# Attention block on one core: half of two units inverted on VectorE, query weights and pair sums moved

## The chip, the cores and the metric

The kernel runs on one core of a Trainium2 chip. The metric is the device time of one execution in microseconds. The engines are named as in the profile: PE (TensorE, matmuls), DVE (VectorE), ACT (ScalarE), POOL (GpSimd) and SP (SyncE, which issues DMAs). PE writes to PSUM, from which DVE and ACT read; POOL works in SBUF alone.

## The reference

Layer 0 is a convolution with a selective scan; layer 1 is an attention and then a recurrence over tokens. The change touches the attention only:

```python
t = t + _L1_attn_ref(_ln_t(t), Wt, Wx, bh, Wa, ba)   # t: 4 batches x 4096 tokens x 128

q = jnp.einsum('bld,ud->blu', x, Wt)                  # u = 32
k = jnp.einsum('bld,ud->blu', x, Wx)
beta = jnp.tanh(q[:, :, None, :] + k[:, None, :, :] + bh)
alpha = jnp.einsum('bsju,u->bsj', beta, Wa[:, 0]) + ba[0]
alpha = jnp.tanh(alpha)
alpha = jax.nn.softmax(alpha, axis=-1)
c_r = jnp.einsum('bsj,bjd->bsd', alpha, x)
```

For each pair of a query and a key the score is a weighted sum of 32 tanh values. There are 4 x 4096 x 4096 such pairs.

## The kernel before, in words

The attention is `_rational`. It groups the 32 units into six sets of five or six. Within a set, the sum of tanh values is one quotient N/D of two sums over products of exponentials, which matmuls form from a query factor `E` and a key factor `F`. So a pair costs six quotients, not 32 tanh. D is the product of `F` and `E` ("lower", tile `pd`), and N that of `F` and `cE`, which is `E` times a constant per row (`weigh`, L1379; the constants hold the factor `LOWER`, 2^-13).

**Tiling.** A block is 512 queries (QB) of one batch against all 4096 keys: 4 batches x 8 blocks = 32 blocks. Its 32 key tiles (`jt`) hold 128 keys each. A key tile has three units, "A", "B1" and "B2" (in odd tiles A, B2, B1), each with two halves (two of the six sets), so a unit is 2 x 512 columns. Unit (30,0) is the A unit of key tile 30, and the numbers 0, 1, 2 are the units' places in the tile.

**The loop over units (L1520 to L1548).** The instructions are written in a fixed order by hand (`manual_schedule`), and every engine takes its own in that order. At step i:

- ACT takes the logarithm of unit i's denominators out of PSUM (Ln, L1524) and then the exponential of unit i-1's negated logarithm (Exp, L1527). Together they invert D.
- DVE multiplies unit i-2 by its numerators, half by half (`times`, L1414: one input in SBUF, one in PSUM).
- POOL adds a B unit's two quotients to those of the tile's A unit (L1533), two adds per key tile.
- At the step in which a tile's first B unit is multiplied, DVE adds the two halves of the tile before into the scores `A` (`whole`, L1518; both inputs and the output in SBUF).
- PE forms the denominators of unit i+2 and the numerators of unit i-1 (L1393).

The buffers that tie these together: two PSUM tiles `pd` for denominators (each a whole unit), three banks `pn` for numerators (each half a unit), one bank `ct` for everything else; four `ra` tiles for A quotients and five `rb` tiles for B quotients.

**Between the units.** The dictionary `between` holds extra steps by (key tile, place), run after that unit's instructions: the norm of the next batch (14 to 23), the last 12 value matmuls of the block before (2 to 13), its closing division (14 to 21, with the residual add L1462 on POOL), the next block's query factors (23 to 26: matmul, maximum on DVE, exponential L1300 on ACT), and in the first block of a batch the transposes of the values (24 to 30).

**The tanh stretch.** At a block's end ACT loads another table and computes tanh and exp of the scores in four parts, the last over key tiles 20 to 31 (L1583, L1584). Before it, DVE weighs the next block's `E` into `cE`. Meanwhile `ahead` does key tile 0 of the next block without ACT: `direct` inverts D on DVE by a reciprocal (L1424) and multiplies by N (L1425). It also forms the first two denominators of key tile 1 (`first`). Then ACT loads its table again (L1266) and the next block's loop starts at key tile 1. At a change of batch the key factor `F` is first made anew (`all_keys`). DMAs of the stage (SP's queue) fetch one block's residual and, up to the third batch, the next batch's tokens.

The functions as they stand:

Of the kernel before, what the change touches and what calls it, by code (L numbers as in the profile page):

```python
# [8 lines left out]
F32 = mybir.dt.float32  # L9
AF = mybir.ActivationFunctionType  # L10
# [5 lines left out]
P = 128  # L16
# [54 lines left out]
LOWER = 2.0**-13  # L71
TOPS = B * 2 * 2 * (L // QB)
# [1169 lines left out]
def _rational(ctx, tc, k, x1, xn1, x2, top, kept, ba):  # L1242
# [14 lines left out]
    rb = ctx.enter_context(tc.tile_pool(name="nrb", bufs=5))  # L1257
    two = ctx.enter_context(tc.tile_pool(name="ntwo", bufs=2))
    fp = ctx.enter_context(tc.tile_pool(name="nf", bufs=1))
# [116 lines left out]
    def weigh(E):  # L1376
        cE = one.tile([P, 2, QB], F32, name="cE")
        for i in range(2):
            nc.vector.tensor_scalar(cE[:, i, :], E[:, i, :], c_n[:, i : i + 1], None, ALU.mult)  # L1379
        return cE  # L1380
# [31 lines left out]
    def times(r, ns):  # L1412
        for a in range(2):
            nc.vector.tensor_tensor(r[:, a, :], r[:, a, :], ns[a], ALU.mult)  # L1414
# [5 lines left out]
    def direct(d, ns, unit, then=None):  # L1420

        r = ratio(unit)
        for a in range(2):
            nc.vector.reciprocal(r[:, a, :], d[:, a, :])  # L1424
            nc.vector.scalar_tensor_tensor(r[:, a, :], r[:, a, :], 1.0 / LOWER, ns[a], ALU.mult, ALU.mult)  # L1425
            if then is not None:
                then()
                then = None
        return r
# [4 lines left out]
    def later(between, jt, pos, steps):  # L1434
        n = 3 * jt + pos
        for go, after in steps:
            between.setdefault(divmod(n + after, 3), []).append(go)
# [53 lines left out]
    for b in range(B):  # L1491
        upcoming = None
        for s in range(nq):
# [11 lines left out]
            if more:  # L1505
                E_next = two.tile([P, 2, QB], F32, name="E")
                of = upcoming if turned else xn
                for i in range(2):
                    later(between, 23 + 2 * i, 2, zip(queries(E_next, of, (s + 1) % nq, i), (0, 1, 2)))
            ln_exp()  # L1510
            units = [(jt, pos, unit) for jt in range(start, JT) for pos, unit in enumerate(order(jt))]
            n = len(units)
            D = dict(enumerate(first))
            N, R = {}, {}

# [4 lines left out]
            for i in range(n + 2):  # L1520
                if i < n:
                    jt, pos, unit = units[i]
                    r = R[jt, pos] = ratio(unit)
                    nc.scalar.activation(r, D.pop(i), AF.Ln, scale=LOWER)  # L1524
                if 1 <= i <= n:
                    r = R[units[i - 1][:2]]
                    nc.scalar.activation(r, r, AF.Exp, scale=-1.0)  # L1527
                if i >= 2:
                    at, p, unit = units[i - 2]
                    r = R[at, p]  # L1530
                    times(r, N.pop(i - 2))
                    if p:
                        nc.gpsimd.tensor_tensor(R[at, 0], R[at, 0], R.pop((at, p)), ALU.add)  # L1533
                    if p == 1 and at > start:
                        whole(at - 1)
                forms = []
                if i + 2 < n:
                    D[i + 2] = pd()
                    forms.append(halves((D[i + 2][:, 0, :], D[i + 2][:, 1, :]), units[i + 2], F, E))
# [12 lines left out]
            if more:  # L1552
                E, cE = E_next, weigh(E_next)
# [7 lines left out]
            held = {}  # L1561

            def ahead(step):
                if not more:
                    if step == 0:
                        whole(JT - 1)
                    return
                if step == 0:
                    held["A"], held["B1"] = lower("A", F, 0, E), lower("B1", F, 0, E)
                    held["A"] = direct(held["A"], upper("A", F, 0, cE), "A", lambda: whole(JT - 1))  # L1570
# [8 lines left out]
                else:  # L1579
                    held["first"] = held["first"], lower("B2", F, 1, E)  # L1580

# [282 lines left out]
```

## Time and profile before

| what | us |
|---|---|
| median of three runs | 10636.88 (10631.07 to 10638.2) |
| the profiled execution's own time | 10622.87 |
| its span, first to last instruction | 10621.1 |
| attention, first weighing to last table load for tanh | 3611.6 to 10357.8 |
| one block early on, table load to table load | 6330.39 to 6538.47: 208.1 |
| one block of the last batch | 9506.21 to 9717.83: 211.6 |
| Ln and Exp on ACT, sum of the four groups' lengths over the kernel | 7425.0 |
| pool adds of quotients (L1533) on POOL | 5000.9, 2.519 each |

The lengths of ACT's rows overlap, since the next instruction is shown as started before the last has ended. Their sum is more than the stage, so ACT's pace is read from starts. In timelines "x2" is two instructions of the same kind in a row, merged, and "[0.49 <-PE pn L1393]" is idle time before the instruction and what ended it.

### The profile page before, as it was taken

The page shows a single profiled execution, that of the slowest core. Times are in us where ns is not written, and L with a number is a line of the kernel's source. Part 1 is how long each engine was busy: PE and PEld are TensorE (multiplying, and loading weights), DVE is VectorE, ACT ScalarE, POOL GpSimd, SP SyncE. Part 2 cuts the span into 40 slices and gives each one's busy share as a digit, 9 for nine tenths or more (in the row PEclk, how much of TensorE's full clock was granted, in tenths as well). Part 3 has the DMA queues.
Part 4 walks back from the last instruction along what each step waited for, and adds up shares of the span by engine and source line. Part 5 has one row for each costly group of instructions (what it writes and reads, how often), then busy time and mean ns, then how long its engine had stood idle before and what let it go on. Part 6 is the DMA issues. An engine that isn't in the chain of part 4 may idle for free.

```text
span 10621.1 us, 110120 instructions
## 1 busy us (share of the span) xinstructions
PE 9213.9 (87%) x35452; PEld 3226.5 (30%) x35452; DVE 9043.7 (85%) x10031; ACT 9094.5 (86%) x10279; POOL 8609.3 (81%) x3686
## 2 busy tenths in 40 slices
PE   7787787787777799999999999999999999999997
PEld 2121221222211233333333333333333333333334
DVE  7999999999999788888888888888888888888882
ACT  4566666766766799999999999999999999999995
POOL 7999899999999777788678778877888777767773
PEclk8898898898888999999999999999999999999998
DMA  6889889888888200000000000000000000000001
GB/s 150 200 191 213 189 193 212 194 197 209 198 199 203 71 4 4 4 4 7 4 4 4 7 4 4 7 4 4 4 7 4 4 3 5 3 3 3 5 2 66
DMA packets 228573, 739.50 MB, mean 70 GB/s; under 512 B 41536, under 2 KB 42368, under 8 KB 226448
## 3 DMA queue, kind: packets, MB, share of 16 engines
q1 hardware_dynamic: 224576, 730.76, 29.2%
q8 instruction: 280, 4.59, 0.2%
q14 instruction: 309, 2.53, 0.1%
q10 hardware_dynamic: 3408, 1.63, 0.1%
HBM read 609.15 MB, written 118.88 MB: 69 GB/s over the span
## 4 chain that ended last, share of the span: by engine, by line
PE 35%; ACT 21%; DVE 5%; issue 5%; POOL 1%; DMA 0%; DVEq 0%; POOLq 0%; ACTq 0%; SPq 0%
PE pd L1393 16%; PE pn L1393 10%; PE ct L1557 6%; ACT rb L1527 6%; ACT rb L1524 6%; ACT ra L1524 2%; ACT A L1583 2%; DVE rb L1414 2%; ACT ra L1527 2%; ACT A L1584 1%; DVE ra L1424 1%; PE vy L1758 1%; POOL ra L1533 0%; DVE cE L1379 0%; ACT E L1300 0%
## 5 line engine op out<-in xcount | busy, mean ns | idle before, releaser
L1533 POOL TENSOR_TENSOR ra<-ra,rb 128x1024 f32<-128x1024 f32 x1986 | 5000.9, 2519 | 813.0 <-ACT rb L1527 446.5
L1393 PE MATMUL pn<-cE,F 32*128 32x512 f32 (+1 forms) x12288 | 4602.5, 643 | 88.3 <-DVE rb L1414 78.0
L1393 PE MATMUL pd<-E,F 32*128 32x512 f32 (+1 forms) x12288 | 4037.8, 650 | 342.9 <-ACT ra L1524 239.8
L1414 DVE TENSOR_TENSOR rb<-rb,pn 128x512 f32<-128x512 f32 x3972 | 2543.4, 682 | 582.4 <-PE pn L1393 576.8
L1527 ACT ACTIVATE rb<-rb 128x1024 f32<-128x1024 f32 x1986 | 2513.6, 1270 | 0.0
L1524 ACT ACTIVATE rb<-pd 128x1024 f32<-128x1024 f32 x1986 | 2443.0, 1230 | 26.9 <-PE pd L1393 24.6
L786 POOL TENSOR_TENSOR dBu<-dtdu,bbcc 128x1024 f32<-128x1024 f32 x1024 | 2391.4, 2365 | 88.8 <-DMA dtdu<-dd 58.2
L1393 PEld LDWEIGHTS pd<-E,F 32*128 32x128 f32 (+1 forms) x12288 | 1209.9, 186 | 2257.2 <-ACT ra L1524 972.1
L1393 PEld LDWEIGHTS pn<-cE,F 32*128 32x128 f32 (+1 forms) x12288 | 1420.9, 186 | 1317.3 <-DVE rb L1414 647.0
L1414 DVE TENSOR_TENSOR ra<-ra,pn 128x512 f32<-128x512 f32 x1986 | 1356.1, 686 | 384.8 <-PE pn L1393 287.4
L826 PE MATMUL py<-h,gather 128*32 128x512 f32 x4096 | 1190.6, 677 | 391.7 <-POOL h L812 372.9
L1527 ACT ACTIVATE ra<-ra 128x1024 f32<-128x1024 f32 x993 | 1258.0, 1267 | 0.0
L1524 ACT ACTIVATE ra<-pd 128x1024 f32<-128x1024 f32 x993 | 1210.4, 1219 | 52.6 <-PE pd L1393 43.7
L781 ACT ACTIVATE pa<-dtdu,a_neg 128x1024 f32<-128x1024 f32 x1024 | 1143.6, 1117 | 34.7 <-DMA dtdu<-dd 11.2
L802 DVE TENSOR_TENSOR_SCAN pa<-pa,carry,dBu 128x1024 f32<-128x1024 f32 x480 | 1125.4, 2345 | 32.3 <-ACT pa L781 22.9
L1557 PE MATMUL ct<-A,xT 128*128 128x512 f32 x2048 | 1046.4, 639 | 10.5 <-ACT A L1584 10.5
L812 POOL TENSOR_TENSOR h<-h,bbcc 128x1024 f32<-128x1024 f32 x381 | 899.3, 2360 | 121.8 <-ACT carry L810 104.9
L810 ACT COPY carry<-pa 128x1 f32<-128x1 f32 x643 | 103.0, 160 | 883.9 <-DVE h L809 883.3
L809 DVE TENSOR_TENSOR h<-pa,bbcc 128x1024 f32<-128x1024 f32 x643 | 787.7, 1225 | 61.7 <-PE py L826 1.7
L1518 DVE TENSOR_TENSOR A<-ra 128x512 f32<-128x512 f32 x993 | 753.9, 759 | 35.9 <-POOL ra L1533 31.6
L802 DVE TENSOR_TENSOR_SCAN h<-pa,carry,dBu 128x1024 f32<-128x1024 f32 x288 | 673.2, 2341 | 21.3 <-PE py L826 10.6
L826 PEld LDWEIGHTS py<-h,gather 128*32 128x32 f32 x4096 | 221.8, 116 | 1255.9 <-issue 529.0
(306 smaller groups left out, 8282.2 us busy)
## 6 DMA issues: line engine op xcount, KB each, us to landing
bbcc<-bcd SPq DMA_DIRECT2D x1024, 256.0 KB, 7.7
dtdu<-ddd SPq DMA_DIRECT2D x1008, 256.0 KB, 7.8
ddd<-dd SPq DMA_DIRECT2D x63, 1024.0 KB, 5.1
src<-src SPq DMA_DIRECT2D x60, 512.0 KB, 9.7
xs<-in_x_dram SPq DMA_DIRECT2D x32, 256.0 KB, 7.3
src<-xs SPq DMA_DIRECT2D x16, 512.0 KB, 6.2
bcd<-bc SPq DMA_DIRECT2D x64, 128.0 KB, 1.9
src<-xsT SPq DMA_DIRECT2D x16, 512.0 KB, 5.4
```

The costliest lines, as they stand in the source:

```text
L781: nc.scalar.activation(dA, its[m].DT[r][:, 0, :], AF.Exp, scale=a)
L786: nc.gpsimd.tensor_tensor(dBu, its[m].DT[r][:, 1, :], its[m].BC[q][:, 0, :], ALU.mult)
L802: nc.vector.tensor_tensor_scan(to[:, step], dA[:, step], live.pop(("dBu", u))[:, step], 0.0 if m % nch == 0 else its[m - 1].carry[:, col : ...
L809: nc.vector.tensor_tensor(h, dA, cc, ALU.mult)
L812: nc.gpsimd.tensor_tensor(h, h, cc, ALU.mult)
L826: nc.tensor.matmul(it.y[to, c], gather, live["h", v][:, c], start=False, stop=(q == QS - 1))
L1393: nc.tensor.matmul(ps[a], F[lo:hi, i, jt * P : (jt + 1) * P], side[lo:hi, i, :], start=True, stop=True)
L1414: nc.vector.tensor_tensor(r[:, a, :], r[:, a, :], ns[a], ALU.mult)
L1524: nc.scalar.activation(r, D.pop(i), AF.Ln, scale=LOWER)
L1527: nc.scalar.activation(r, r, AF.Exp, scale=-1.0)
L1533: nc.gpsimd.tensor_tensor(R[at, 0], R[at, 0], R.pop((at, p)), ALU.add)
L1557: nc.tensor.matmul(ct, xT[:, jt, :], A[:, jt, :], start=(jt == 0), stop=(jt == JT - 1))
```

## The change

1. **Half of unit (30,0) on DVE** (`SHARED`), in all blocks but the first of each batch and the last of all. After unit (28,0) PE forms the unit's first denominators in the `ct` bank instead of the `pd` tile; after (28,1), (28,2), (29,0) and (29,1) DVE inverts them, 128 columns at a time. In the loop ACT's Ln and Exp then take the other half alone (512 columns for 1024), and `times` multiplies the first half by N and 1/LOWER (`scalar_tensor_tensor` instead of `tensor_tensor`).
2. **Half of unit (1,0) on DVE in the tanh stretch**, in all blocks but the first of each batch: the last step of `ahead` adds a reciprocal of 512 columns of the first denominators.
3. **`weigh` moved** from the block's end to `between` after unit (26,2), into a second `cE` buffer.
4. **Pair sums moved**: `whole` of tile 30 from the last tile's steps into `direct`, after its first half; `whole` of tile 31 after the second half instead of the first.
5. **Buffers**: four `rb` tiles instead of five, two `cE` tiles instead of one; the pool of `F` is opened before that of `xn`, `E` and `cE`.

No matmul, DMA or POOL instruction is added or taken away.

```diff
@@ -69,6 +69,8 @@
 NOW = 20
 REACH = 21.0
 LOWER = 2.0**-13
+SHARED = ((30, 0),)
+SHARED_BY = 2
 TOPS = B * 2 * 2 * (L // QB)
 MEET = 5e-7
 KEPT = 6 * P + 4
@@ -1254,9 +1256,9 @@
     one = ctx.enter_context(tc.tile_pool(name="none", bufs=1))
     sb = ctx.enter_context(tc.tile_pool(name="nsb", bufs=2))
     ra = ctx.enter_context(tc.tile_pool(name="nra", bufs=4))
-    rb = ctx.enter_context(tc.tile_pool(name="nrb", bufs=5))
+    rb = ctx.enter_context(tc.tile_pool(name="nrb", bufs=4))
+    fp = ctx.enter_context(tc.tile_pool(name="nf", bufs=1))
     two = ctx.enter_context(tc.tile_pool(name="ntwo", bufs=2))
-    fp = ctx.enter_context(tc.tile_pool(name="nf", bufs=1))
     kp = ctx.enter_context(tc.tile_pool(name="nk", bufs=1))
     psD = ctx.enter_context(tc.tile_pool(name="npsD", bufs=2, space=PSUM))
     psN = ctx.enter_context(tc.tile_pool(name="npsN", bufs=3, space=PSUM))
@@ -1374,7 +1376,7 @@
         return exponent(pw, w_q, xn[:, s * QB : (s + 1) * QB], i, E[:, i, :])
 
     def weigh(E):
-        cE = one.tile([P, 2, QB], F32, name="cE")
+        cE = two.tile([P, 2, QB], F32, name="cE")
         for i in range(2):
             nc.vector.tensor_scalar(cE[:, i, :], E[:, i, :], c_n[:, i : i + 1], None, ALU.mult)
         return cE
@@ -1409,23 +1411,25 @@
     def upper(unit, F, jt, cE):
         return products((pn(), pn()), unit, F, jt, cE)
 
-    def times(r, ns):
+    def times(r, ns, inverted=()):
         for a in range(2):
-            nc.vector.tensor_tensor(r[:, a, :], r[:, a, :], ns[a], ALU.mult)
+            if a in inverted:
+                nc.vector.scalar_tensor_tensor(r[:, a, :], r[:, a, :], 1.0 / LOWER, ns[a], ALU.mult, ALU.mult)
+            else:
+                nc.vector.tensor_tensor(r[:, a, :], r[:, a, :], ns[a], ALU.mult)
 
     def ratio(unit):
         pool, tag = (ra, "ra") if unit == "A" else (rb, "rb")
         return pool.tile([P, 2, QB], F32, name=tag, tag=tag)
 
-    def direct(d, ns, unit, then=None):
+    def direct(d, ns, unit, then=(None, None)):
 
         r = ratio(unit)
         for a in range(2):
             nc.vector.reciprocal(r[:, a, :], d[:, a, :])
             nc.vector.scalar_tensor_tensor(r[:, a, :], r[:, a, :], 1.0 / LOWER, ns[a], ALU.mult, ALU.mult)
-            if then is not None:
-                then()
-                then = None
+            if then[a] is not None:
+                then[a]()
         return r
 
     def order(jt):
@@ -1507,11 +1511,28 @@
                 of = upcoming if turned else xn
                 for i in range(2):
                     later(between, 23 + 2 * i, 2, zip(queries(E_next, of, (s + 1) % nq, i), (0, 1, 2)))
+                later(between, 26, 2, [(lambda E_next=E_next: held.update(cE=weigh(E_next)), 0)])
             ln_exp()
+            held = {}
             units = [(jt, pos, unit) for jt in range(start, JT) for pos, unit in enumerate(order(jt))]
             n = len(units)
-            D = dict(enumerate(first))
+            D = dict(enumerate(first[:2]))
             N, R = {}, {}
+            shared = {}
+            if len(first) > 2:
+                shared[units[0][:2]] = {"r": first[2]}
+            for jt, pos in SHARED if more and s else ():
+                mine = shared[jt, pos] = {}
+
+                def inverse(h=mine, jt=jt, unit=order(jt)[pos], F=F, E=E):
+                    h["d"], h["r"] = pw(), ratio(unit)
+                    halves((h["d"], None), (jt, 0, unit), F, E)[0]()
+
+                def invert(k, h=mine):
+                    cols = slice(k * P, (k + 1) * P)
+                    nc.vector.reciprocal(h["r"][:, 0, cols], h["d"][:, cols])
+
+                later(between, jt - SHARED_BY, pos, [(inverse, 0)] + [(lambda k=k, invert=invert: invert(k), k + 1) for k in range(QB // P)])
 
             def whole(jt, A=A, R=R):
                 r = R.pop((jt, 0))
@@ -1520,23 +1541,27 @@
             for i in range(n + 2):
                 if i < n:
                     jt, pos, unit = units[i]
-                    r = R[jt, pos] = ratio(unit)
-                    nc.scalar.activation(r, D.pop(i), AF.Ln, scale=LOWER)
+                    half = (jt, pos) in shared
+                    r = R[jt, pos] = shared[jt, pos]["r"] if half else ratio(unit)
+                    rest = slice(1, 2) if half else slice(0, 2)
+                    nc.scalar.activation(r[:, rest, :], D.pop(i)[:, rest, :], AF.Ln, scale=LOWER)
                 if 1 <= i <= n:
                     r = R[units[i - 1][:2]]
-                    nc.scalar.activation(r, r, AF.Exp, scale=-1.0)
+                    rest = slice(1, 2) if units[i - 1][:2] in shared else slice(0, 2)
+                    nc.scalar.activation(r[:, rest, :], r[:, rest, :], AF.Exp, scale=-1.0)
                 if i >= 2:
                     at, p, unit = units[i - 2]
                     r = R[at, p]
-                    times(r, N.pop(i - 2))
+                    times(r, N.pop(i - 2), (0,) if (at, p) in shared else ())
                     if p:
                         nc.gpsimd.tensor_tensor(R[at, 0], R[at, 0], R.pop((at, p)), ALU.add)
-                    if p == 1 and at > start:
+                    if p == 1 and start < at < JT - 1:
                         whole(at - 1)
                 forms = []
                 if i + 2 < n:
                     D[i + 2] = pd()
-                    forms.append(halves((D[i + 2][:, 0, :], D[i + 2][:, 1, :]), units[i + 2], F, E))
+                    both = halves((D[i + 2][:, 0, :], D[i + 2][:, 1, :]), units[i + 2], F, E)
+                    forms.append([lambda: None, both[1]] if units[i + 2][:2] in shared else both)
                 if 1 <= i <= n:
                     N[i - 1] = pn(), pn()
                     forms.append(halves(N[i - 1], units[i - 1], F, cE))
@@ -1550,24 +1575,23 @@
             assert not between
 
             if more:
-                E, cE = E_next, weigh(E_next)
+                E, cE = E_next, held["cE"]
             ct = pw()
 
             def weighted(jt, ct=ct, xT=xT):
                 nc.tensor.matmul(ct, xT[:, jt, :], A[:, jt, :], start=(jt == 0), stop=(jt == JT - 1))
 
 
-
-            held = {}
 
             def ahead(step):
                 if not more:
                     if step == 0:
+                        whole(JT - 2)
                         whole(JT - 1)
                     return
                 if step == 0:
                     held["A"], held["B1"] = lower("A", F, 0, E), lower("B1", F, 0, E)
-                    held["A"] = direct(held["A"], upper("A", F, 0, cE), "A", lambda: whole(JT - 1))
+                    held["A"] = direct(held["A"], upper("A", F, 0, cE), "A", (lambda: whole(JT - 2), lambda: whole(JT - 1)))
                 elif step == 1:
                     held["B2"] = lower("B2", F, 0, E)
                     held["B1"] = direct(held["B1"], upper("B1", F, 0, cE), "B1")
@@ -1578,6 +1602,10 @@
                     nc.gpsimd.tensor_tensor(held["A"], held["A"], r, ALU.add)
                 else:
                     held["first"] = held["first"], lower("B2", F, 1, E)
+                    if not turned:
+                        r = ratio("A")
+                        held["first"] += (r,)
+                        nc.vector.reciprocal(r[:, 0, :], held["first"][0][:, 0, :])
 
             for i, (lo, hi) in enumerate(PARTS if more else LAST_PARTS):
                 nc.scalar.activation(A[:, lo:hi, :], A[:, lo:hi, :], AF.Tanh, bias=b_a)
```

## The prediction

> **What bounds the kernel now.** I read the page's slices first, then ACT's order of time in one block, then DVE's and POOL's beside it. The slices from the 14th on are the attention:
>
> ```profile
> ACT  4566666766766799999999999999999999999995
> POOL 7999899999999777788678778877888777767773
> ```
>
> ACT is full, and POOL is nearly so. The timeline of ACT (start, length) shows its real pace:
>
> ```profile
> 6472.81 1.49 ACT L1524 ACTIVATE ra<-pd 128x1024 f32<-128x1024 f32 x1
> ...
> 6478.36 1.52 ACT L1524 ACTIVATE ra<-pd 128x1024 f32<-128x1024 f32 x1
> ...
> 6486.25 1.02 ACT L1524 ACTIVATE ra<-pd 128x1024 f32<-128x1024 f32 x1 [0.65 <-PE pd L1393]
> ...
> 6507.10 0.68 ACT L1300 ACTIVATE E<-ct 128x512 f32<-128x512 f32 x1
> 6507.58 1.11 ACT L1524 ACTIVATE rb<-pd 128x1024 f32<-128x1024 f32 x1
> ```
>
> Lengths overlap, so starts count: a key tile (six ACT instructions) takes 5.55 us, 0.925 us each; a 512-column one takes 0.48. So ACT's instructions set the pace, except where one key tile took 7.89 us (6478.36 to 6486.25), 2.34 too many. DVE and POOL there, by timeline:
>
> ```profile
> 6477.95 1.26 POOL L1462 TENSOR_TENSOR xr<-xr,rec 128x512 f32<-128x512 f32 x1
> 6479.18 4.67 POOL L1533 TENSOR_TENSOR ra<-ra,rb 128x1024 f32<-128x1024 f32 x2
> 6485.76 2.36 POOL L1533 TENSOR_TENSOR ra<-ra,rb 128x1024 f32<-128x1024 f32 x1 [1.92 <-ACT ct L1328]
> ```
> ```profile
> 6479.40 1.28 DVE L1414 TENSOR_TENSOR rb<-rb,pn 128x512 f32<-128x512 f32 x2 [0.49 <-PE pn L1393]
> 6481.57 2.82 DVE L1518 TENSOR_TENSOR A<-ra 128x512 f32<-128x512 f32 x1 [0.88 <-POOL ra L1533]
> 6484.32 1.27 DVE L1414 TENSOR_TENSOR rb<-rb,pn 128x512 f32<-128x512 f32 x2
> ```
>
> The residual add (1.26 us) made POOL late. `whole` (L1518), which must wait for a tile's second pool add, came free just as POOL, whose next add was ready, began it. `whole` then took 2.82 us instead of its usual 0.69: it ended 0.54 after that add (6483.85). DVE reads and writes only SBUF there, as POOL does, and gets no turn until POOL's instruction ends. Behind it stood the numerator products, whose three PSUM buffers PE needs before it forms the next denominators, so ACT stopped. This recurs in every block at key tile 22.
>
> **The change, part by part**
>
> *Two weighings moved (L1379).* At the block's end they take
>
> ```profile
> 6533.81 10.57 POOL L1533 TENSOR_TENSOR ra<-ra,rb 128x1024 f32<-128x1024 f32 x4 [0.46 <-ACT rb L1527]
> ```
> ```profile
> 6540.82 3.85 DVE L1379 TENSOR_SCALAR cE<-E,consts 128x512 f32<-128x512 f32 x2
> ```
>
> The second ends at 6544.67, 0.29 after POOL's last add (6544.38); alone, in the first block, one takes 0.48. So they too wait for POOL. Their new place is after unit (26,2) is issued, behind the ra pair at 6507.61, in the rows
>
> ```profile
> 6505.45 5.12 POOL L1533 TENSOR_TENSOR ra<-ra,rb 128x1024 f32<-128x1024 f32 x2 [0.49 <-ACT rb L1527]
> 6511.46 5.12 POOL L1533 TENSOR_TENSOR ra<-ra,rb 128x1024 f32<-128x1024 f32 x2 [0.89 <-DVE rb L1414]
> ```
> ```profile
> 6507.61 1.49 DVE L1414 TENSOR_TENSOR ra<-ra,pn 128x512 f32<-128x512 f32 x2
> 6510.03 1.28 DVE L1414 TENSOR_TENSOR rb<-rb,pn 128x512 f32<-128x512 f32 x2 [0.93 <-PE pn L1393]
> ...
> 6515.66 1.29 DVE L1414 TENSOR_TENSOR rb<-rb,pn 128x512 f32<-128x512 f32 x2 [0.49 <-PE pn L1393]
> 6516.86 0.69 DVE L1518 TENSOR_TENSOR A<-ra 128x512 f32<-128x512 f32 x1
> ```
>
> The first is issued at 6509.0, waits for POOL until 6510.57, ends at 6510.86; the second finds POOL idle (its next add needs the product behind it on DVE) and costs 0.39 (0.48 less the overlap of neighbours). The product of 6510.03 starts at 6511.17: 1.14 late. DVE makes that up in one tile (idle 0.21 + 0.40 + 0.49). POOL doesn't: its pair starts 1.14 late and ends at 6517.72, not 6516.58. `whole` would start at 6516.86 and must now wait for 6517.72; POOL's next add has been ready since 6516.95. That is tile 22 again, at tile 28: `whole` ends near 6520.6, 3 us late. Nearest row: +2.34 per block. Below: if `whole` slips in first, 0. Above: 3.30 + 0.81, as in the last batch, where the clock fell as well (9655.97 to 9664.82, the next tile 6.36). I take 2.34, in 31 blocks: +72.5. Its old cost, 3.77 us of DVE, goes to the third part.
>
> *Half of unit (30,0), 27 blocks.* ACT saves 2 x (0.925 - 0.48) = 0.90. DVE gains four 128-column reciprocals, 0.95 each (L1454 row), 0.87 net with overlap: 3.48 us in two tiles that have 2.2 idle. Excess 1.3; a denominator is ready 1.3 before ACT wants it (PE ends at 6521.07, Ln starts at 6522.38). Alone that about cancels the gain; behind a DVE already late it costs more. Ends: -0.90 (all hidden) and +1.5 (excess stands, no gain left); I take +0.3, nearer to the excess: +8. The multiply that follows keeps its length (L1425 0.688, L1414 0.685).
>
> *Half of the next block's first unit, 28 blocks.* ACT again saves 0.90, if DVE is done in time. Its chain now runs from 6540.82 to 6569.63 and ACT's next Ln starts at 6570.18. It loses 3.77 (weighing), gains one pair sum (0.60) and one reciprocal (3.35 + 0.1). But it can't start 3.77 sooner: the denominators it inverts are formed from 6540.11 on at half clock and arrive near 6542.2. So 6542.2 + 25.0 + 0.6 + 3.5 = 6571.3: the reciprocal ends 1.1 after ACT has begun, holding the PSUM buffer that PE's third unit takes at 6571.26 today. Gain 0.1 of 0.90: -3. Ends: -0.90 (chain earlier) and +0.5 (DVE arrives late).
>
> *At nothing.* Pair sums 30 and 31 move into the tanh stage, where the last tanh, which reads them, starts at 6558.11, some 6 us after they end; without that cover 0.6 each. Four rb buffers for five: unit (26,2)'s buffer is free at 6516.58 and wanted at 6518.68; with POOL 1.14 late 0.96 remains; beyond it each us of lateness is one of ACT's. The shared matmul is issued two tiles earlier into a bank whose users ended at 6507.78: same count. POOL gets no instruction and keeps its order; no DMA is added or moved, so SP's queue is untouched. Second cE buffer: no wait on old readers.
>
> *The clock.* Windows of the trace (length, PE busy, other engines, granted clock):
>
> ```profile
> 6535.08:6538.49 3.41, 3.27 (x10) 1.23 (x10) 2.63 (x5) 3.39 (x5) 3.33 (x2) 1.00 0.00 0
> 6538.47:6548.71 10.24, 10.24 (x17) 2.82 (x17) 9.99 (x9) 10.16 (x5) 5.80 (x3) 0.50 0.01 2
> 9661.68:9668.51 6.83, 5.84 (x19) 2.16 (x20) 4.42 (x8) 4.09 (x5) 2.35 (x1) 0.50 0.00 0
> ```
>
> After a stretch with few, narrow matmuls the clock is halved. Within 5 us of the blocked `whole` of tile 22 this befell 12 of 31 blocks, at 1.75 each (3.30 + 0.81 against 2.34). A second starved place at the same rate: 12 x 1.75 = +21; ends 0 and +54 (all 31). The Trainium skill ("TensorE: Matmul & The Clock Gate", What's actually happening) names an idle window of 3413 ns as what closes the gate. By that rule a 2 us starvation would not close it and the 21 would go. The trace differs: the clock fell after a window with PE busy 3.27 of 3.41.
>
> The blocks pull into step with these windows: 208.1 us from table load to table load early (6538.47 to 6746.58), 211.6 in the last batch (9506.21 to 9717.83). The 31 steps from 3804.34 to 10357.76 are 6553.4, of which 65 are extra work (three changes of batch, 20 each, and the last block's 5). Were every step 211.6, they would be 6624.6, or +71; the terms above make +98.5. I take the middle: -13.
>
> Sum: 72.5 + 8 - 3 + 21 - 13 = +85 us. Profiled execution 10622.87 (span 10621.1): 10708. The median shown is 14.0 above it: **10722**.
>
> **Rivals.** (1) Faster: `whole` isn't blocked. Point: POOL less than 0.37 late at tile 26 (6516.95 less 6516.58), as if the weighings passed beside POOL's add. For it: the four rows need exact timing. Against: the 34 `whole`s that met an add at its start took 2.8, and at every block's end both weighings ended 0.3 after an add. With both halves gained, 55 x 0.90 = -49.5. If the steps settle at 208.2 instead, near today's commonest, the 31 make 6519, or -34: 10603 (10587 to 10625). (2) No blocking, but the inversions overload DVE and late denominators stall ACT: 27 x 1.5 + 28 x 0.5 = +55: 10692. (3) The gain is real but swallowed by the windows: 10637.
>
> **How the numbers follow.** Chances: forecast 0.62, all slower; (1) 0.22, of it 0.19 faster and 0.03 same; (2) 0.10, slower; (3) 0.06, half same, half faster. Faster 0.22, same 0.06, slower 0.72; 0.2% (21 us) is about what a measurement can tell. The forecast's own range is 10660 (blocking at 2.34, both gains) to 10800 (clock halved in each block, +54, and inversions at +1.5, +40). The range reaches down into (1): 10590.
>
> **What would show it.** In the profile after: L1518 rows of 2.8 us twice a block; POOL idle 1.9 after tile 27's first add; L1379 near 1.9 and 0.5; key tile 28 near 7.9 on ACT. If L1518 is long only once a block, (1) or (2) holds; an Ln wait on PE at the block's third unit shows the third part right.

## The result, and the profile after

The changed kernel takes **10899.1 us** (median of six, 10878.69 to 10911.63) against 10633.97 (10627.29 to 10639.3) for the kernel before in the same comparison: a ratio of **1.0247, 95% interval 1.0236 to 1.0258**. That is +265 us. The forecast was +85, and its range ended at 10800. The direction was right, the size was not.

The page of the changed kernel, slices and two groups (in the slices, the attention begins at the 14th):

```profile
POOL 7999999999999667776777677767776677767773
...
PEclk8898898898888999999999999999999999999998
...
L1547 ACT ACTIVATE ra<-pd 128x1024 f32<-128x1024 f32 (+1 forms) x993 | 1139.6, 1148 | 329.4 <-DVE ra L1608 149.4
```

POOL does the same adds and is less full than before: it waits. ACT's Ln of the A units (L1547, L1524 before) now waits 329.4 us in all, where it waited 52.6; nearly half of that is for L1608, the reciprocal that was added to the tanh stretch. In the changed kernel `whole` is L1539, `weigh` L1381, `times` L1419 and POOL's add L1557.

Two measures make the rest readable, both from the two profiled executions. A step is the time from one block's table load for tanh to the next block's. The 31 steps together were 6553.4 us and are 6836.6. The part of it from the table load of the tanh to the next block's first Ln was 31.71 in each block but those at a change of batch; it is 37.04 on average now. 28 x 5.33 = 149, and 3.7 at each of the three changes of batch, make 160 us in the tanh stretch. The other 123 lie in the loop over units: by ACT's starts, key tiles 27 and 28 take 54 us more over the 31 steps, tiles 2 to 7 26, tiles 1 and 22 to 25 17 each, tiles 29 and 30 11.

The place the prediction spoke of most, in one block (first DVE, then POOL, by timeline):

```profile
6625.47 1.49 DVE L1419 TENSOR_TENSOR ra<-ra,pn 128x512 f32<-128x512 f32 x2
6626.87 2.22 DVE L1381 TENSOR_SCALAR cE<-E,consts 128x512 f32<-128x512 f32 x2
6629.01 1.27 DVE L1419 TENSOR_TENSOR rb<-rb,pn 128x512 f32<-128x512 f32 x2
...
6636.85 0.69 DVE L1539 TENSOR_TENSOR A<-ra 128x512 f32<-128x512 f32 x1
```
```profile
6623.30 5.11 POOL L1557 TENSOR_TENSOR ra<-ra,rb 128x1024 f32<-128x1024 f32 x2 [0.44 <-ACT rb L1551]
6630.43 5.11 POOL L1557 TENSOR_TENSOR ra<-ra,rb 128x1024 f32<-128x1024 f32 x2 [2.02 <-DVE rb L1419]
```

The two weighings take 2.22 together (2.3 expected), end 0.68 after POOL's add, and POOL then idles 2.02 instead of 0.89. That step came out as written. The next one, the pair sum blocked in key tile 28, came in 15 of the 31 blocks only; in this one that pair sum takes 0.69 (6636.85). What follows in the same block was not foreseen:

```profile
6652.34 1.28 DVE L1419 TENSOR_TENSOR rb<-rb,pn 128x512 f32<-128x512 f32 x2 [0.43 <-PE pn L1395]
6654.04 2.82 DVE L1539 TENSOR_TENSOR A<-ra 128x512 f32<-128x512 f32 x1 [0.42 <-POOL ra L1557]
6656.79 1.27 DVE L1419 TENSOR_TENSOR rb<-rb,pn 128x512 f32<-128x512 f32 x2
...
6665.61 3.36 DVE L1429 RECIPROCAL ra<-pd 128x512 f32<-128x512 f32 x1 [1.33 <-PE pd L1395]
...
6691.72 3.35 DVE L1608 RECIPROCAL ra<-pd 128x512 f32<-128x512 f32 x1
```
```profile
6688.26 1.28 ACT L1268 ACT_TABLE_LOAD   x1
6695.17 0.60 ACT L1547 ACTIVATE ra<-pd 128x512 f32<-128x512 f32 x1 [5.62 <-DVE ra L1608]
```

A pair sum is blocked in key tile 31 (2.82 us); this happens in 26 of the 31 blocks. DVE's chain of the tanh stretch starts at 6665.61, 7.8 us behind the table load of 6657.85, where the prediction had reckoned with 3.7. The added reciprocal ends at 6695.07, and ACT's first Ln, free since 6689.54, starts 0.10 later. Over all blocks but those at a change of batch, the two go together: in the five whose pair sum of tile 31 is not blocked, the chain starts 2.8 to 4.7 behind the table load and the first Ln comes at 31.8 to 34.3; in the other 23 the chain starts at 7.1 to 8.7 and Ln comes at 36.7 to 38.3.

### The profile page after: what moved, and what is told of

Same layout as the page of the kernel before. It is cut to its first block, busy times and chain, and to the rows that moved or that the text cites. A ratio compares the mean times of both kernels' runs of the same rounds, so it can differ in the third digit from the quotient of the medians.

```text
span 10909.9 us, 109630 instructions
## 1 busy us (share of the span) xinstructions
PE 9470.3 (87%) x35452; PEld 3245.8 (30%) x35452; DVE 9282.8 (85%) x10167; ACT 9070.1 (83%) x10279; POOL 8578.5 (79%) x3686
## 4 chain that ended last, share of the span: by engine, by line
PE 40%; ACT 13%; DVE 10%; issue 3%; POOL 0%; DMA 0%; DVEq 0%; ACTq 0%; SPq 0%; POOLq 0%
PE pd L1395 19%; PE pn L1395 15%; ACT rb L1551 4%; PE ct L1582 4%; ACT rb L1547 4%; DVE rb L1429 3%; ACT ra L1547 2%; ACT ra L1551 2%; DVE rb L1419 2%; DVE ra L1429 1%; DVE ra L1608 1%; DVE A L1539 1%; DVE rb L1430 1%; PE vy L1786 1%; DVE ra L1533 0%
## 5 line engine op out<-in xcount | busy, mean ns | idle before, releaser
L1557 POOL TENSOR_TENSOR ra<-ra,rb 128x1024 f32<-128x1024 f32 x1986 | 4969.9, 2504 | 1147.1 <-DVE rb L1419 806.3
L1395 PE MATMUL pn<-cE,F 32*128 32x512 f32 (+1 forms) x12288 | 4874.7, 664 | 206.4 <-DVE rb L1419 204.2
L1395 PE MATMUL pd<-E,F 32*128 32x512 f32 (+1 forms) x12234 | 4294.6, 666 | 259.3 <-ACT ra L1547 215.8
L1419 DVE TENSOR_TENSOR rb<-rb,pn 128x512 f32<-128x512 f32 x3972 | 2539.7, 680 | 585.9 <-PE pn L1395 561.5
L1551 ACT ACTIVATE rb<-rb 128x1024 f32<-128x1024 f32 x1986 | 2412.4, 1217 | 0.0
L1547 ACT ACTIVATE rb<-pd 128x1024 f32<-128x1024 f32 x1986 | 2342.3, 1179 | 41.2 <-PE pd L1395 24.4
L1395 PEld LDWEIGHTS pn<-cE,F 32*128 32x128 f32 (+1 forms) x12288 | 1497.0, 192 | 1669.7 <-DVE rb L1419 1032.6
L1395 PEld LDWEIGHTS pd<-E,F 32*128 32x128 f32 (+1 forms) x12234 | 1275.0, 191 | 2158.6 <-ACT ra L1547 896.8
L1419 DVE TENSOR_TENSOR ra<-ra,pn 128x512 f32<-128x512 f32 x1931 | 1312.5, 684 | 313.9 <-PE pn L1395 237.8
L1547 ACT ACTIVATE ra<-pd 128x1024 f32<-128x1024 f32 (+1 forms) x993 | 1139.6, 1148 | 329.4 <-DVE ra L1608 149.4
L1551 ACT ACTIVATE ra<-ra 128x1024 f32<-128x1024 f32 (+1 forms) x993 | 1184.3, 1193 | 0.0
L1539 DVE TENSOR_TENSOR A<-ra 128x512 f32<-128x512 f32 x993 | 874.7, 881 | 52.8 <-POOL ra L1557 49.8
```

What stands on the lines that cost most here:

```text
L1395: nc.tensor.matmul(ps[a], F[lo:hi, i, jt * P : (jt + 1) * P], side[lo:hi, i, :], start=True, stop=True)
L1539: nc.vector.tensor_tensor(A[:, jt, :], r[:, 0, :], r[:, 1, :], ALU.add)
L1547: nc.scalar.activation(r[:, rest, :], D.pop(i)[:, rest, :], AF.Ln, scale=LOWER)
L1551: nc.scalar.activation(r[:, rest, :], r[:, rest, :], AF.Exp, scale=-1.0)
```

## The experiments

The letters of theories here are those of the expectations; each letter holds for the runs beside which it stands. Two theories stood first. **P** (the port): every added DVE instruction makes POOL late, and a late POOL blocks pair sums; the loss lies in the loop. **S** (the stretch): the loss lies in the tanh stretch, through the reciprocal there. "Long pair sums" counts `whole` over 1.5 us in the 31 steps; "half clock" is the time in them at a granted clock of 0.5; the last column is the mean step inside the first, second, third and last batch. A pair sum is named by the key tile at which ACT stands when it runs. Each ratio is to the kernel before as timed in the same comparison (medians of 10626 to 10634). The traces also differ by up to 18 us ahead of the attention, which no edit touches, so a difference of 10 or 20 us in the second column can't be put down to the loop without the last column.

| kernel | median us | ratio to before, 95% | long pair sums | half clock us | steps us |
|---|---|---|---|---|---|
| before | 10634 | | 33 | 365 | 208.7, 208.8, 208.5, 212.4 |
| changed | 10899.1 | 1.0236 to 1.0258 | 90 | 782 | 217.6, 218.6, 220.2, 219.9 |
| e1 without the reciprocal in the stretch | 10811.8 | 1.0149 to 1.0183 | 84 | 625 | 215.0, 215.0, 214.7, 218.1 |
| e2 without half of (30,0) | 10883.9 | 1.0222 to 1.0256 | 98 | 802 | 219.4, 217.2, 218.6, 219.0 |
| e3 moves alone | 10791.5 | 1.0141 to 1.0175 | 91 | 597 | 214.9, 215.1, 215.1, 215.0 |
| e4 reciprocal in a tile of its own | 10903.7 | 1.0242 to 1.0276 | 90 | 754 | 218.1, 218.0, 218.0, 221.4 |
| e5 moves, weighings on ACT | 10732.9 | 1.0076 to 1.0109 | 64 | 546 | 212.7, 213.3, 211.5, 216.3 |
| e6 before, residual add behind the loop | **10580.1** | 0.9936 to 0.9969 | 0 | 297 | 208.1, 208.4, 208.5, 207.8 |
| e7 before, four `rb` | 10647.5 | 1.0010 to 1.0029 | 37 | 365 | 209.4, 208.3, 209.3, 212.4 |
| e8 before, weighings moved, four `rb` | 10799.5 | 1.0142 to 1.0176 | 99 | 645 | 214.0, 214.5, 214.4, 215.5 |
| e9 moves and e6 | 10722.1 | 1.0070 to 1.0103 | 55 | 532 | 212.5, 213.6, 213.6, 210.7 |
| e10 changed and e6 | 10817.6 | 1.0154 to 1.0188 | 49 | 601 | 215.6, 216.4, 217.5, 214.8 |
| e11 e6 and 1 us of ACT in the stretch | 10613.1 | 0.9974 to 0.9993 | 3 | 311 | 209.5, 210.0, 210.4, 207.8 |
| e12 e6, weighings behind the first reciprocal | **10575.1** | 0.9929 to 0.9962 | 4 | 294 | 208.4, 208.6, 208.3, 206.1 |
| e13 e12 and the reciprocal in the stretch | 10579.0 | 0.9943 to 0.9971 | 2 | 314 | 208.2, 208.7, 208.5, 206.1 |
| e14 before and the reciprocal in the stretch | 10705.5 | 1.0061 to 1.0095 | 37 | 437 | 211.7, 211.7, 211.9, 213.9 |
| e15 before and half of (30,0) | 10728.1 | 1.0079 to 1.0112 | 68 | 539 | 212.0, 211.8, 211.4, 216.2 |
| e16 e12 and both inversions | 10673.0 | 1.0028 to 1.0062 | 27 | 505 | 211.2, 211.1, 211.1, 209.8 |

### Taking parts away: e1, e2, e3

```diff
# e1 (e3 has this and the next)
-                    if not turned:
-                        r = ratio("A")
-                        held["first"] += (r,)
-                        nc.vector.reciprocal(r[:, 0, :], held["first"][0][:, 0, :])
# e2
-SHARED = ((30, 0),)
+SHARED = ()
```

> The changed kernel without the reciprocal in the tanh stretch (its second part); half of unit (30,0), the moved weighings and pair sums stay. Theory S (the stretch): most of the loss arises where ACT's first Ln of a block waits for that reciprocal (5.6 us idle in a block of the changed kernel, and 1.8 more in key tile 1). Then the step from table load to the first Ln falls back from about 37.5 to 31.7 and the median to about 10705 (31 blocks at 2.2 above the kernel before). Theory P (the port, as predicted): the loss is DVE held up behind POOL near key tile 28; then little changes: about 10870.

> The changed kernel without the half of unit (30,0); the reciprocal in the tanh stretch stays. Theory S: DVE then enters the stretch some 4 us earlier, as in the first block of each batch, where the first Ln comes 34.2 after the table load instead of 37.5: about 10810. Theory P: the four inversions only add to a DVE already late; without them about 10860. If the inversions were the whole cause: 10640 to 10700.

> The changed kernel without both inversions: only the weighings after unit (26,2), the pair sums and the buffers are moved. Theory P prices this at 1.9 us in each of 31 blocks in key tiles 27 and 28 (as the changed kernel shows) and a clock halved more often: 10695 to 10730. Theory S says the same of the loop, but a shorter DVE chain in the stretch gains nothing since ACT sets its end: 10690 to 10700. If the blocked pair sum needs the inversions to happen: 10630.

The sizes were missed. The moves alone, with nothing inverted, cost 160 us, the largest part. On top of them half of (30,0) costs 20 (e1 less e3) and the reciprocal 87 (the changed kernel less e1). So P has the larger share and S the smaller. The reciprocal's 87 are less than the 160 by which the stretch grew: without it (e1) key tile 1 takes 7.10 us on average instead of 6.14. In e3's 31 steps, key tiles 27 and 28 take 66 us more than before, tiles 29 and 30 57, tiles 22 to 25 19 and tile 1 16. How that comes about can be read in one block of e3, DVE and POOL by timeline:

```profile
6371.50 2.82 DVE L1539 TENSOR_TENSOR A<-ra 128x512 f32<-128x512 f32 x1 [0.30 <-POOL ra L1557]
6374.24 1.27 DVE L1419 TENSOR_TENSOR rb<-rb,pn 128x512 f32<-128x512 f32 x2
...
6385.47 2.82 DVE L1539 TENSOR_TENSOR A<-ra 128x512 f32<-128x512 f32 x1 [0.30 <-POOL ra L1557]
```
```profile
6366.63 7.13 POOL L1557 TENSOR_TENSOR ra<-ra,rb 128x1024 f32<-128x1024 f32 x3 [2.31 <-DVE rb L1419]
6375.68 2.35 POOL L1557 TENSOR_TENSOR ra<-ra,rb 128x1024 f32<-128x1024 f32 x1 [1.92 <-DVE rb L1419]
6380.31 7.44 POOL L1557 TENSOR_TENSOR ra<-ra,rb 128x1024 f32<-128x1024 f32 x3 [2.28 <-DVE rb L1419]
```

The pair sum blocked in tile 28 (6371.50) holds back the product that POOL needs next, so POOL idles 1.92, then 2.28. It is late again, and the pair sum two tiles on (6385.47) is blocked in the same way. Here one blocked pair sum begets the next: in 27 of the 31 blocks of e3 one is blocked in tile 28 or 29 and one more in tile 30 or 31. It need not: the one of tile 22 is followed by another in the last block alone of the kernel before. What decides was not tested. Both stretches lose PE's clock too (windows of e3: length, busy time of PE, its weight loads, DVE, ACT and POOL, clock):

```profile
6371.49:6374.90 3.41, 1.43 (x5) 0.39 (x4) 3.40 (x3) 3.06 (x4) 2.28 (x1) 0.99 0.00 0
6374.90:6378.30 3.40, 3.33 (x12) 1.12 (x15) 1.90 (x4) 1.18 (x2) 2.35 (x1) 0.51 0.00 0
6385.08:6388.50 3.42, 1.73 (x6) 0.30 (x4) 3.12 (x3) 3.35 (x4) 2.67 (x2) 1.00 0.02 5
6388.50:6395.30 6.80, 6.35 (x20) 2.16 (x20) 4.39 (x8) 4.13 (x5) 3.03 (x2) 0.50 0.00 0
```

While DVE stood, PE was busy 1.43 and 1.73 of 3.41 us; the next 3.4 and 6.8 us ran at half clock. With that the two tiles take 8.35 and 8.36 us instead of 5.55. No run separates what the slow clock costs from what the blocked pair sum costs. The Trainium skill ("TensorE: Matmul & The Clock Gate", What's actually happening) lets an idle window close the gate; here the clock fell after windows in which PE was half busy, and in the row that the prediction shows after one with 3.27 of 3.41 us busy, so the busy share alone doesn't tell when. The page's free-running window of 3413 ns agrees with the trace: the 94 half-clock stretches in e3's steps are whole multiples of 3.41 us long, 53 of them a single one.

### Is it the port? e5, e8, e7, e6, e9

```diff
# e5, on e3
-            nc.vector.tensor_scalar(cE[:, i, :], E[:, i, :], c_n[:, i : i + 1], None, ALU.mult)
+            nc.scalar.activation(cE[:, i, :], E[:, i, :], AF.Copy, scale=c_n[:, i : i + 1])
# e8, on before (with it two cE buffers; four rb for room)
+                later(between, 26, 2, [(lambda E_next=E_next: held.update(cE=weigh(E_next)), 0)])
...
-                E, cE = E_next, weigh(E_next)
+                E, cE = E_next, held["cE"]
# e7, on before
-    rb = ctx.enter_context(tc.tile_pool(name="nrb", bufs=5))
+    rb = ctx.enter_context(tc.tile_pool(name="nrb", bufs=4))
# e6, on before (e9: the same on e3; e10: on the changed kernel)
+            if parts == 1:
+                store()
+
+        def store():
             nc.gpsimd.tensor_tensor(xr, xr, held["rec"], ALU.add)
             nc.sync.dma_start(x2[b, :, blocks[s]], xr)
 
+        if parts > 1:
+            stored.append(store)
...
             assert not between
+            for go in stored:
+                go()
+            stored.clear()
```

> The kernel of the moves alone (no inversion), with the two weighings in the same place, but done by ACT as a copy with a scale, so that DVE no longer stands behind POOL's add there. Theory W (the weighings on DVE, held by POOL's add, make POOL's next pair late, and that blocks the pair sums of key tiles 28 and 30 in a chain): no pair sum of 2.8 us after key tile 22, the step back at 208 to 209; ACT's two copies of about 0.5 in 31 blocks add 30: 10645 to 10680. Theory M (the moved pair sums or the fewer buffers do it, whoever weighs): long pair sums at 28 and 30 stay, 10790 to 10830.

> The kernel before with the weighings moved to key tile 26 on DVE (second buffer for them, four rb buffers to make room), the pair sums 30 and 31 where they were. Theory W: the whole loss of the moves, 10770 to 10810, with long pair sums at 28 and 30 in nearly each block. Theory M: 10640 to 10710.

> The kernel before with four rb buffers for five, nothing else. Both theories: 10632, within 10; the buffer of unit (22,1) and (22,2) may be awaited at key tile 22, where POOL is 2 us late: then up to 31 x 0.5 = 15 more.

> The kernel before with the residual add (POOL, 1.26 us, at key tile 21) and its DMA issued behind the loop. If a late POOL is what blocks the pair sum of key tile 22: no pair sum of 2.8 us there any more, key tile 22 near 5.6 instead of 7.9, 31 x 2.34 = 73 less, and the halved clock of 12 blocks (21) with it, less what the locking to whole clock windows takes back: 10530 to 10580. If POOL is late for another reason (the ACT rows of the residual stage ahead of it), nothing changes: 10632. In the block's end the add stands behind POOL's last add, 0.7 to 1.3 us, in front of the tanh stretch's adds, which have slack.

> The kernel of the moves alone, with the residual add behind the loop, so that POOL isn't late at key tile 21 and the pair sum of key tile 22 isn't blocked. Theory W (the moved weighings make POOL late by themselves): pair sums blocked at 28 and then 30 or 31 in most blocks as before, the step at 62 or 63 clock windows (211.6 to 215.0): 10670 to 10780. Theory C (the weighings tip over only since POOL is late already from key tile 22): no blocked pair sum at 28, the step at 61 windows: 10570 to 10610.

e8 is a hit: the moved weighings alone (with four `rb`) give the whole loss of the moves, 10799.5; the pair sums' new places do nothing measurable. Four `rb` buffers alone are 20 us slower (e7), where the prediction had nothing; but e7's trace puts 10 of them into the steps and 12 ahead of the attention, and shows no Ln that waits for POOL to free a buffer, so whether the missing buffer itself costs anything is open. No run moves the weighings with five `rb` tiles.

e6 shows the mechanism from the other side. DVE and POOL around key tile 22:

```profile
6471.51 1.28 DVE L1414 TENSOR_TENSOR rb<-rb,pn 128x512 f32<-128x512 f32 x2 [0.49 <-PE pn L1393]
6472.71 0.68 DVE L1526 TENSOR_TENSOR A<-ra 128x512 f32<-128x512 f32 x1
```
```profile
6467.36 5.19 POOL L1541 TENSOR_TENSOR ra<-ra,rb 128x1024 f32<-128x1024 f32 x2 [0.22 <-ACT rb L1535]
6472.93 5.11 POOL L1541 TENSOR_TENSOR ra<-ra,rb 128x1024 f32<-128x1024 f32 x2 [0.38 <-ACT rb L1535]
```

With the residual add out of the way POOL's pair ends at 6472.55, before DVE is done with its products, and `whole` slips in ahead of the next add: 0.68 instead of 2.82. No long pair sum is left in 31 steps, and the kernel is 0.5% **faster** than before. The Trainium skill ("SBUF — State Buffer", Who interferes with whom) says that a DVE instruction with two SBUF inputs contends with a POOL one that reads SBUF, under an exclusive lock. The rows agree: 2.82 against 0.68 for the same instruction, by who starts first.

e5 missed both forecasts. No weighing is on DVE, yet 64 pair sums are long. ACT's two copies make key tile 26 7.25 us instead of 6.03, which is 39 us in all, POOL waits for ACT instead, and in 19 of the 31 blocks a pair sum is blocked in tile 29 (31 more of the 64 are those of tile 22). So a pair sum can be blocked without a weighing on DVE; what the three cases share is that POOL comes late, by a residual add (e6 undoes it), by DVE (e8) or by ACT (e5).

e9 decides that the weighings suffice. Without the lateness of tile 21 they still block two pair sums in tiles 28 to 31 of most blocks, and the time is 142 us above e6.

### The tanh stretch and the inversions: e4, e14, e13, e15, e16, e10

```diff
# e4, on the changed kernel: the reciprocal into a tile that nothing else uses
-                        r = ratio("A")
+                        r = one.tile([P, QB], F32, name="rh")
# e14, on before: part 2 of the change alone. e15: part 1 alone
# e12, on e6 (e13: with part 2; e16: with parts 1 and 2)
-                E, cE = E_next, weigh(E_next)
+                E = E_next
...
+                    nc.vector.reciprocal(r[:, 0, :], d[:, 0, :])
+                    cE = weigh(E)
+                    ns = upper("A", F, 0, cE)
+                    nc.vector.reciprocal(r[:, 1, :], d[:, 1, :])
```

> The changed kernel, but the reciprocal in the tanh stretch is written to a tile of its own instead of the first half of the quotient tile whose second half ACT's Ln writes. If the first Ln waits because both write one tile, it now comes 31.7 after the table load, and the wait moves to the third unit, whose denominators need the PSUM buffer that the reciprocal reads until about 37: ACT gains some 2 us a block, about 10850. If it waits for the denominators' PSUM tile itself, nothing changes: 10900.

> The kernel before with the reciprocal in the tanh stretch alone (half of the next block's first unit, 28 blocks), nothing moved. In the trace of before DVE's chain there ends 0.55 us ahead of the first Ln. Theory D (the term costs since DVE comes late out of the loop in the changed kernel): little here beyond the 2.9 us by which the reciprocal now ends behind that Ln; if Ln waits for it as in the changed kernel, 2.9 - 0.9 = 2.0 in 28 blocks, 56, and up to one clock window per block (95): 10680 to 10730. Theory N (Ln need not wait when DVE isn't late): the forecast's own term, 10605 to 10650.

> The kernel with the residual add behind the loop and the weighings behind the first reciprocal (10575), with the reciprocal in the tanh stretch added. There the chain of DVE ends 28.0 to 29.5 us behind the table load, so the reciprocal ends at 31.5 to 33, and Ln is due at 31.7. Theory D: it waits at most 1.3 and saves 0.9: 10550 to 10590. If the term costs what it cost in the changed kernel, whenever the chain ends (Ln waiting for something else of DVE): 10640 to 10670.

> The kernel before with half of unit (30,0) inverted on DVE alone, nothing moved. Theory K (the four inversions in tiles 28 and 29 make POOL late by themselves): pair sums blocked at 29 to 31 in most of the 27 blocks, one clock window more, 10690 to 10730. Theory L (they tip POOL over only where the weighings have made it late): no blocked pair sum besides 22, ACT saves up to 0.9 in 27 blocks: 10605 to 10640.

> The kernel with the residual add behind the loop and the weighings behind the first reciprocal (10575), with both inversions. Theories D and L together: 10530 to 10590. Theories D and K: 10630 to 10680.

> The whole changed kernel with the residual add behind the loop. Theory W: pair sums still blocked at 28 and 31, the stage of the tanh still near 37, one clock window less than the changed kernel or none: 10780 to 10900. Theory C: the weighings and the inversions pass, only the reciprocal in the tanh stretch can cost: 10560 to 10700.

e14 hits theory D: 79 us for the reciprocal alone. ACT's order of time in one block of it, and DVE's:

```profile
6388.52 1.28 ACT L1268 ACT_TABLE_LOAD   x1
6392.61 0.60 ACT L1546 ACTIVATE ra<-pd 128x512 f32<-128x512 f32 x1 [2.81 <-DVE ra L1606]
```
```profile
6389.15 3.35 DVE L1606 RECIPROCAL ra<-pd 128x512 f32<-128x512 f32 x1
```

Ln of the other half starts 0.11 after the reciprocal ends, as in the changed kernel: it waits for it, although it needs no result of it. A quotient tile of its own changed nothing (e4, 10903.7), so the shared quotient tile isn't why; what the wait stands for was not settled (the tile of denominators, of which each reads a half, was not tried). e13 is the counter-test: where DVE's chain starts earlier, Ln starts 0.12 after the reciprocal's end (the profile names PE as what released it), but that is only 0.45 late, and the time is e12's (10579.0 against 10575.1, intervals overlapping). ACT's Ln and DVE's reciprocal in one block of e13:

```profile
6361.89 0.60 ACT L1554 ACTIVATE ra<-pd 128x512 f32<-128x512 f32 x1 [0.45 <-PE pd L1395]
```
```profile
6358.42 3.35 DVE L1626 RECIPROCAL ra<-pd 128x512 f32<-128x512 f32 x1
```

So the reciprocal costs by how late it ends. It gains nothing either: key tile 1 falls from 5.85 to 3.77 us in many blocks, while the stretch grows by 1.16 on average.

e15 hits theory K: half of (30,0) alone costs 102 us. The four inversions fill DVE, so POOL's products come late; in key tile 31 `whole` waits 0.42 for POOL's pair and meets its next add, in 26 of the 27 blocks that share (30,0) (one block, first DVE, then ACT):

```profile
6351.68 0.95 DVE L1532 RECIPROCAL ra<-ct 128x128 f32<-128x128 f32 x1
...
6360.39 2.83 DVE L1538 TENSOR_TENSOR A<-ra 128x512 f32<-128x512 f32 x1 [0.42 <-POOL ra L1556]
...
6373.91 3.35 DVE L1429 RECIPROCAL ra<-pd 128x512 f32<-128x512 f32 x1
```
```profile
6364.19 1.28 ACT L1605 ACT_TABLE_LOAD   x1
...
6400.52 1.02 ACT L1546 ACTIVATE rb<-pd 128x1024 f32<-128x1024 f32 x1 [3.60 <-PE pd L1395]
```

Key tiles 27 to 31 lose nothing by it in sum (ACT gains in tile 30), but DVE's chain starts 9.7 us behind the table load, where it was 6.1, and key tile 1, where Ln then waits for PE (3.60 here), takes over 8 us in most blocks: 78 of the 105 us by which e15's steps are longer. e16 confirms both on the best base: 98 us more than e12, with a pair sum blocked in key tile 31 of each of the 27 blocks that share (30,0) and a stretch of 37.0 on average (e13: 32.9). e10 lies as its theory W says: 82 us better than the changed kernel, still 184 worse than before.

### Whole clock windows: e11, e12

```diff
# e11, on e6: nothing is changed by the copy
+                if more and i + 1 == len(PARTS):
+                    nc.scalar.activation(A[:, NOW:NOW + 2, :], A[:, NOW:NOW + 2, :], AF.Copy)
```

> The kernel before with the residual add behind the loop (10580), and one ACT copy of 128x1024 in place (1.0 us, nothing is changed by it) at the end of each tanh stretch, 31 times. Theory L (the steps are whole clock windows): the copy vanishes in the wait of key tile 1 for PE, the mean step stays near 208.2 = 61 windows, 10575 to 10595. If the step follows ACT's work: 31 x 1.0 more, 10605 to 10620.

> The kernel before with the residual add behind the loop (10580) and the two weighings, still at the block's end, issued behind the first reciprocal of the tanh stretch instead of ahead of it: that one reads PSUM and needs not wait for POOL, and the weighings then find POOL's last adds done. They took 3.9 us of DVE, should take 0.9; the chain of reciprocals starts near 3 us sooner, PE's idle stretch of 5.2 us behind it shrinks to about 2, so that its clock isn't halved there. Theory L (the halved clock of the tanh stretch sets the step to 61 whole windows, with key tile 1 waiting for PE by up to 2.45): the step falls to the 207.4 of the blocks without that wait, 31 x 0.8 = 25 less: 10545 to 10565. If the clock is halved there all the same, the step stays at 208.2: 10570 to 10590.

Some steps stand at whole multiples of 3.413 us: 208.2 (61), 211.6 (62), 215.0 (63) and 218.5 (64). The clearest are in the last batch, where five steps in a row are 211.62 to 211.68 before and five are 208.18 to 208.21 in e6. Of all 486 single steps inside batches (the last block's left out), 173 lie within 0.25 of a multiple, where chance would give some 70. e6 took 1.26 us out of key tile 22 in the first three batches, and the mean step fell there by 0.55, 0.40 and 0.09 only: most steps there are 207.4 or 209.8, and key tile 1 is longer in the latter. Theory L, that the steps are held at whole windows, is only half right, and the time of e11 (10613.1) lies in the range of its rival. In the last batch of e11 (ACT, first; e6 below it) the added 1.06 us vanish in the wait of tile 1 for PE, and the step stays at 208.2:

```profile
9546.48 1.06 ACT L1597 ACTIVATE A<-A 128x1024 f32<-128x1024 f32 x1
...
9551.14 1.02 ACT L1532 ACTIVATE rb<-pd 128x1024 f32<-128x1024 f32 x1 [1.26 <-PE pd L1393]
```
```profile
9517.04 1.02 ACT L1532 ACTIVATE rb<-pd 128x1024 f32<-128x1024 f32 x1 [2.45 <-PE pd L1393]
```

In the other three batches the steps grew by 1.4, 1.6 and 1.9 and no longer fit a window (two of those blocks, of 215.2 and 213.5, had a long pair sum besides), and the total rose by 33. That this is 31 x 1.06 is chance, since the last batch did not grow. As far as these rows show, a step is held where PE, on a halved clock, is the last to be ready. e12 cannot be told from e6 (10575.1 and 10580.1, overlapping intervals); its last batch went to 206.1, so the hold was lifted there. Its median is the lowest measured here, 0.55% under before.

## Why the prediction failed

The sum had 85 and the runs 265. Of the 180 that are missing, the reciprocal in the stretch has about 90, the weighings 67, half of unit (30,0) behind the moves 12, and the subtraction for whole windows 13. Three steps failed, in the order of the sum:

- **"2.34 per block: +72.5" (the weighings).** The mechanism was right: weighings held, POOL idle 2.02, and where the moves stand alone (e3), a `whole` of 2.82 in tile 28 or 29 in 27 of 31 blocks. The step that failed is that the loss was priced as one event. Key tiles 27 and 28 cost 66 us in e3, near the 72.5; but POOL is late again behind them, and the second event at 30 or 31 (57 us in tiles 29 and 30) was left out: 91 long pair sums in e3 against 33. Measured: +160, for +93.5 with the clock term. The trace of before had shown the chain in its last block, in key tiles 25 and 27:

```profile
10313.80 2.82 DVE L1518 TENSOR_TENSOR A<-ra 128x512 f32<-128x512 f32 x1 [0.31 <-POOL ra L1533]
...
10327.73 2.83 DVE L1518 TENSOR_TENSOR A<-ra 128x512 f32<-128x512 f32 x1 [0.31 <-POOL ra L1533]
```

- **"Half of unit (30,0): +8."** Measured: +102 alone, +20 behind the moves. The step that failed is the price: the inversions were weighed as time on DVE and on ACT, not for what they do to POOL's turn, which blocks the pair sum of tile 31. The upper end, +1.5 a block (40 in all), was far too low for e15.
- **"Half of the next block's first unit: -3."** Measured: +79 alone, +87 in company. Two readings failed. The chain was taken to start 3.7 behind the table load; with the pair sum of tile 31 blocked it starts at 7.1 to 8.7. And Ln was taken to run beside a late reciprocal; it starts 0.10 after its end in the changed kernel and 0.11 in e14.
- **"The clock, +21" and "the steps, -13."** The half clock more than doubled, from 365 to 782 us in the 31 steps; what that cost by itself no run shows. The pull to whole windows was used to shrink the sum to near 62 windows, and the steps went on to means of 217.6 to 220.2, about 64. Nothing in the sum could tell which multiple.
- **"At nothing": four `rb`.** +20 (1.0010 to 1.0029), of which the trace of e7 shows 10 in the steps and no wait for a buffer; the term stays open. The pair sums moved into the stretch did cost nothing that e8 and e3 can tell apart.
- **Rivals.** (1) was wrong in both halves: the pair sum is blocked, and neither half unit yields anything by itself. (2) named the inversions on DVE, at 55 for both; the runs say 102 and 79.

The terms don't add: 172 (e8), 102 and 79 alone make 353, together 265. In the traces part of the difference is in key tile 1, which takes 36 us more over the 31 steps in e8, 78 in e15 and only 17 in the changed kernel, whose first Ln is late already.

## What to carry to other kernels

Price an instruction added to a nearly full engine by whom it makes late, and follow that lateness until it is worked off: where an engine's lateness blocks the one that feeds it, one event can repeat. Look in the trace of before for the place where the chain already runs, the last block or an irregular one. And the cure is worth more than the change: putting the one instruction that made POOL late behind the loop gave 0.5%, where the change lost 2.5%.

## What was not expected of the hardware

- PE's clock fell after windows of 3.41 us in which PE was busy 1.43 or 1.73 us (e3), and after one with 3.27 (before); no window needed to be idle.
- Steps of some 210 us settled on whole multiples of 3.413 us in the last batch, where PE at half clock is the last to be ready: five steps at 211.62 to 211.68 before, five at 208.18 to 208.21 in e6, and 1.06 us of added work on ACT left that batch at 208.2.
- The same DVE addition took 0.68 or 2.82 us by whether it started just ahead of POOL's add or just behind it.
